# Decoder layer: queries of three kv groups by a seven-product block scheme, weights scaled by a two-scalar instruction

## The chip, the core and the metric

The kernel runs on one core of a Trainium2 chip. The metric is the device time of one launch in microseconds (us). A core has five engines with a queue each: PE (matrix products into PSUM), DVE (VectorE), ACT (ScalarE), POOL (GpSimd, which works on SBUF) and SP, which here issues the DMAs. Each queue runs in its order and waits on semaphores.

## The reference

One decoder layer on `x` of 8 x 128 tokens of 512 columns: causal self-attention with 32 query heads in 8 kv groups of 4, then attention of each sequence to a context, then a gated feed-forward part with 4-bit weights. The self-attention views the 1024 rows of `x` as they come:

```python
q = (hidden_states @ w_q).reshape(B, S, Hkv, g, D)
k = (hidden_states @ w_k).reshape(B, S, Hkv, D)
v = (hidden_states @ w_v).reshape(B, S, Hkv, D)
scores = jnp.einsum('bqhgd,bkhd->bhgqk', q, k) * scale
scores = jnp.where(causal, scores, -jnp.inf)
probs = jax.nn.softmax(scores.astype(jnp.float32), axis=-1).astype(q.dtype)
attn = jnp.einsum('bhgqk,bkhd->bqhgd', probs, v)
return attn @ w_o
x = x + _L0_attn_ref(_layernorm(x, axis=-1), w_q, w_k, w_v, w_o)
x = x + _L0_xattn_ref(ctx_4096, ctx_4096, _layernorm(x, axis=-1))
x = x + _L0_ffn_ref(_layernorm(x, axis=-1), ...)
```

(The kernel has the shapes of the reference's arguments as given: 8 sequences of 128 rows.) Only the projections `q`, `k`, `v`, their weights and the dequantised zeros are touched here.

## The kernel before

**Numbers as pairs.** Every f32 operand of a product is split into two 16-bit parts, hi and lo (`split`, L115: ACT casts to hi, then another engine subtracts for lo). A product of two pairs takes three matmuls, hi*hi, hi*lo, lo*hi (`mm3`, L158). Weights are first scaled by a power of two, so that the 16-bit range holds them: `sumsq` (L242, ACT) and `scales` (L270, one small matmul into bank "a" and a few DVE instructions) find the factor, and `convert` (L348) applies it on POOL (`tensor_tensor` with a broadcast factor, L356), casts on ACT and subtracts on POOL.

**Tokens.** `begin` (L830) loads `x`, normalises it and writes `hT[part][half]`, the normalised tokens transposed, columns of 512 tokens in each of two halves, 4 contraction tiles (KT) of 128 rows. Half 0 is also kept in f32, `h32`, in memory that the feed-forward weights take later.

**Units and steps.** Attention runs over units (kv group g, half), 16 of them, of four sequences each: 64 steps. In step i, `step` (L1368) traces the scores of step i+1 (`att_s`, bank "s"), the projections for the unit of step i+5 (`proj_piece`: k at its first step, one query head a step by `proj_q`, values in two of the four steps, all in bank "j"), the output product of step i-1 (`att_o`, bank "o", added into `xr` by DVE at L665) and the probability product of step i (`att_v`, bank "a"). One `proj_q` is 4 contraction tiles x 3 = 12 matmuls of 128x512, then an ACT cast and a DVE subtraction out of PSUM. PSUM has 8 banks, two for each letter.

**Softmax of one step.** DVE reduces scores out of PSUM (L611), ACT exponentiates (L568), POOL scales by the reciprocal sums (L578, L625), ACT and POOL split into `pb` (L116, L119), SP issues the DMA that transposes `pb` into `pt` (L639); `att_v` waits for `pt`.

**Weights to come.** `todo` holds for each step the loads (`fetch_wq`, `fetch_wk`, `fetch_wv`, `fetch_wo`), squares, factors and splits of later groups. Steps 8 on also dequantise one chunk of the feed-forward weights each (`dequant`). Query weights of a group come as one load of 1 MB into one buffer; k and v weights have buffers of their own.

**Order.** Instructions are traced in the order above; a list scheduler of the framework then orders each engine's queue by its own model of time. `in_order` pins the traced order in `begin` and in the last steps.

## Time and profile before

| what | before |
|---|---|
| median of 3 runs (lowest to highest) | 660.35 us (658.78 to 661.13) |
| span of the profiled execution (the page gives no other time of it) | 659.3 us |
| instructions | 12426 |
| query matmuls of 128x512: L162, L163, L164 | 252 each, 379 to 381 ns a record |
| output-product matmuls: L162, L163, L164 | 256 each, 379 ns a record |
| POOL scalings `rawq`, `rawo`, `rawk`, `rawv` (L356), 128x512 | 28, 30, 7 and 6, at 1048, 1053, 1040 and 1037 ns |
| POOL lo parts `wql`, `wol`, `wkl`, `wvl` (L119) | 1167, 1179, 1155 and 1200 ns |
| granted TensorE clock, mean | 0.995 |
| DMA moved | 69.34 MB, mean 105 GB/s |

How to read the profile: each engine's busy time is the sum of its records; matmul records overlap, since the next matmul enters the array before the one ahead has drained, so the distance between two starts is what a matmul costs and the record's length is its latency. A line of a group gives the code line, the engine, the operation, the tiles it writes and reads with their shapes, the count, then busy time, mean duration, and the idle time before it with what ended that.

### The profile page before, as it was taken

The numbers are of one execution on the slowest core, as the hardware profiler recorded it, in microseconds if no ns is written. First come the engines' busy times: TensorE is split into PE (matmuls) and PEld (weight loads), VectorE is DVE, ScalarE is ACT, GpSimd is POOL, SyncE is SP. The second block draws the span as 40 slices with busy tenths as digits, with TensorE's granted clock in tenths as the row PEclk, the third lists the DMA queues.
The fourth block names the chain that finished last, engine by engine and source line by source line (L and its number), as shares of the span: only waits on it lengthen the run. The fifth ranks groups of instructions, "written<-read, shape, count | busy, mean of one in ns | idle before, by whom it ended". The sixth has DMA issues, their size and how long they took to land.

```text
span 659.3 us, 12426 instructions
## 1 busy us (share of the span) xinstructions
PE 630.6 (96%) x3992; PEld 341.9 (52%) x3992; DVE 469.9 (71%) x1474; ACT 440.4 (67%) x1238; POOL 395.8 (60%) x586
## 2 busy tenths in 40 slices
PE   8789999899999999999999999899998988999996
PEld 5455545455655555565555565456554444445443
DVE  6845786656767776675778565677776768988986
ACT  5676677465758574666677565976566578867674
POOL 7757497664747795556588597663576247622521
PEclk9999999999999999999999999999999999999998
DMA  9277244945553755455547514242544243112002
GB/s 316 54 174 146 84 46 133 229 105 158 121 157 80 192 130 153 109 152 140 144 112 163 149 37 120 46 103 57 90 76 70 41 86 55 22 27 65 1 1 64
DMA packets 117773, 69.34 MB, mean 105 GB/s; under 512 B 84190, under 2 KB 100593, under 8 KB 117708
## 3 DMA queue, kind: packets, MB, share of 16 engines
q1 hardware_dynamic: 117708, 68.55, 43.7%
q8 instruction: 31, 0.51, 0.3%
q14 instruction: 34, 0.28, 0.1%
HBM read 42.12 MB, written 2.20 MB: 67 GB/s over the span
## 4 chain that ended last, share of the span: by engine, by line
PE 56%; POOL 13%; DMA 10%; DVE 8%; issue 7%; ACT 5%; SPq 1%; DVEq 0%; POOLq 0%; ACTq 0%
PE ps_c L1184 6%; PE ps_c L1185 6%; PE ps_o L164 5%; PE ps_o L162 5%; PE ps_o L163 5%; PE ps_q L163 5%; PE ps_q L162 5%; PE ps_q L164 5%; DMA pt<-pb 3%; DMA rawq<-in_L_attn_w_q_dram 3%; POOL pb L119 3%; DMA rawo<-in_L_attn_w_o_dram 2%; POOL s L625 2%; POOL wql L119 1%; POOL rawo L356 1%
## 5 line engine op out<-in xcount | busy, mean ns | idle before, releaser
L568 ACT ACTIVATE s<-s,negm 128x64 f32<-128x64 f32 (+1 forms) x256 | 93.1, 365 | 31.6 <-DVE negm L611 31.3
L162 PE MATMUL ps_o<-woh,ah 128*128 128x512 f16 x256 | 97.1, 379 | 3.2 <-ACT ah L116 3.2
L162 PE MATMUL ps_q<-hT,wqh 128*128 128x512 f16 (+1 forms) x260 | 98.2, 378 | 1.7 <-DVE ql L119 1.7
L163 PE MATMUL ps_q<-hT,wqh 128*128 128x512 f16 (+1 forms) x260 | 98.2, 378 | 0.0
L164 PE MATMUL ps_q<-hT,wql 128*128 128x512 f16 (+1 forms) x260 | 98.0, 377 | 0.0
L164 PE MATMUL ps_o<-woh,al 128*128 128x512 f16 x256 | 96.9, 379 | 0.6 <-DVE al L119 0.6
L163 PE MATMUL ps_o<-wol,ah 128*128 128x512 f16 x256 | 97.0, 379 | 0.0
L119 POOL TENSOR_TENSOR pb<-s,pb 128x256 f16<-128x256 f32 (+1 forms) x128 | 71.7, 575 | 14.8 <-ACT pb L116 12.4
L665 DVE SCALAR_TENSOR_TENSOR xr<-ps_o,unsc,xr 128x512 f32<-128x512 f32 x64 | 47.8, 747 | 42.5 <-PE ps_o L164 41.9
L611 DVE CUSTOM_DVE_ANT_0 s<-ps_sc,mask,soft 128x64 f32<-128x64 f32 (+1 forms) x256 | 66.9, 309 | 4.3 <-PE ps_sc L164 2.0
L578 POOL TENSOR_SCALAR rec<-rec 128x4 f32<-128x4 f32 x64 | 14.8, 231 | 90.1 <-DVE rec L576 87.4
L625 POOL TENSOR_TENSOR s<-s,rec 128x128 f32<-128x128 f32 (+1 forms) x128 | 64.3, 523 | 4.5
L116 ACT CAST pb<-s 128x256 f16<-128x256 f32 (+1 forms) x128 | 43.0, 350 | 33.7 <-POOL s L625 30.0
L119 DVE TENSOR_TENSOR ql<-ps_q,qh 128x512 f16<-128x512 f32 x64 | 43.9, 686 | 28.8 <-ACT qh L116 28.6
L116 ACT CAST ah<-ps_at 128x512 f16<-128x512 f32 x64 | 37.1, 581 | 23.3 <-PE ps_at L164 10.1
L119 DVE TENSOR_TENSOR al<-ps_at,ah 128x512 f16<-128x512 f32 x64 | 43.7, 683 | 7.0 <-ACT ah L116 6.6
L568 ACT ACTIVATION_READ_ACCUMULATOR s<-s,negm 128x1 f32 x256 | 48.1, 188 | 0.0
L116 ACT CAST qh<-ps_q 128x512 f16<-128x512 f32 x64 | 36.7, 573 | 14.0 <-PE ps_q L164 12.5
L1197 DVE TENSOR_SCALAR ps_c<-ps_c,rTg 128x512 f32<-128x512 f32 (+1 forms) x56 | 40.7, 750 | 7.1 <-PE ps_c L1185 6.8
L356 POOL TENSOR_TENSOR rawo<-rawo,sco 128x512 f32<-128x512 f32 x30 | 31.4, 1053 | 22.5 <-DVE sco L312 20.3
L1195 ACT ACTIVATE ps_c<-ps_c,rTu 128x512 f32<-128x512 f32 (+1 forms) x57 | 36.3, 659 | 11.3 <-PE ps_c L1185 9.2
L164 PE MATMUL ps_sc<-k,ql 128*128 128x64 f16 (+1 forms) x256 | 42.7, 206 | 0.5 <-DVE ql L119 0.5
(243 smaller groups left out, 1728.9 us busy)
## 6 DMA issues: line engine op xcount, KB each, us to landing
rawq<-in_L_attn_w_q_dram SPq DMA_DIRECT2D x8, 1024.0 KB
rawo<-in_L_attn_w_o_dram SPq DMA_DIRECT2D x8, 1024.0 KB, 6.0
zi<-zd SPq DMA_DIRECT2D x26, 256.0 KB, 4.1
vd<-v SPq DMA_DIRECT2D x64, 64.0 KB, 2.6
qr<-_L_ffn_down_qweight_dram SPq DMA_DIRECT2D x10, 256.0 KB
xr<-in_x_dram SPq DMA_DIRECT2D x8, 256.0 KB, 7.7
rawk<-in_L_attn_w_k_dram SPq DMA_DIRECT2D x8, 256.0 KB, 4.5
rawv<-in_L_attn_w_v_dram SPq DMA_DIRECT2D x4, 512.0 KB
```

The source lines that it names most:

```text
L116: a = nc.scalar.copy(hi, src)
L119: b = (lo_eng or nc.vector).tensor_tensor(lo, src, hi, ALU.subtract)
L162: nc.tensor.matmul(ps, lh, rh, start=start and i == 0, stop=False)
L163: nc.tensor.matmul(ps, lh, rl, start=False, stop=False)
L164: nc.tensor.matmul(ps, ll, rh, start=False, stop=stop and i == n - 1)
L568: exp = nc.scalar.activation(v, v, AF.Exp, bias=negm[:, j : j + 1], scale=-1.0, accum_out=sums[:, j : j + 1],)
L611: nc.vector.tensor_tensor_reduce(view, flat(ps, cols[j]), masks[j // 2], soft_t[g][:, j % 2 : j % 2 + 1], BIG, ALU.add, ALU.min, negm,)
L625: mul = nc.gpsimd.tensor_tensor(v, v, rec[:, 2 * k : 2 * k + 2].unsqueeze(2).to_broadcast([P, 2, (k + 1) * HQ]), ALU.mult,)
L665: return nc.vector.scalar_tensor_tensor(xr[b], ps, unsc_t[g], xr[b], ALU.mult, ALU.add)
L1184: nc.tensor.matmul(ps, lh, rh, start=r == 0, stop=False, skip_group_check=r > 0)
L1185: nc.tensor.matmul(ps, lh, rl, start=False, stop=True, skip_group_check=r > 0)
L1197: nc.vector.tensor_scalar(ps, ps, sc, None, ALU.mult)
```

## The change

Three things are changed.

**Seven products.** For kv groups 3, 4 and 5 (`FAST`), the queries of two heads (a pair p of a group) over both halves are seen as a 2x2 block product: two heads by two halves of the contraction (2 of the 4 tiles each), times two halves of the contraction by two token halves. Instead of eight block products of 6 matmuls (`proj_q` four times), `fast_q` makes seven, with sums of weight blocks (`fast_prep`, part 2, four DVE additions; Z0 and Z1 are their pairs) and sums of token blocks (`t_part`, once, in steps 8 to 11; kept as pairs in `tT`). Partial products are shared: an ACT copy puts half of c11 into the bank of `u`, on which PE goes on adding, and DVE adds `s5`, the fifth product, to `u` twice. `fast_q` is cut in four parts by its yields, and `fast_steps` runs them in successive steps, 8g-9 to 8g-6 for the first pair and 8g-5 to 8g-2 for the second (the third part of the very first pair comes in step 18, with the fourth). All four query tiles of a pair come in these steps, half 1 long before its use, so those of the second pair's half 1 are kept in a pool of their own (`tp`, beside `tT`).

**Scaling.** `scaled` applies a weight's factor on POOL by `tensor_scalar` with two per-partition scalars, `nil` (zero, added) and the factor, in place of the `tensor_tensor`.

**Room and order for it.** Scores have one bank "s", and "b" is the bank of `u`; where no `u` is live, scores alternate between both (tag "sb"). Query weights come in two loads of 512 KB, k and v weights share one buffer, and their loads, squares and splits move; group 1's k load moves within `begin`. Value projections of later groups go to bank "o", one in each of 8 steps. Work tiles of the start (`warm`, `hb`, `h`, the first k weights, zeros and scales) move into memory of the feed-forward weights (`lent`), the zeros are stored as 16-bit numbers, both masks share a tile, and `junk` is 8 bits wide.

```diff
-    BANKS = {"j": 2, "s": 2, "a": 2, "o": 2}
+    BANKS = {"j": 2, "s": 1, "a": 2, "o": 2, "b": 1}
+
+    flip = [0]
     def bank(tag, shape, name):
+        if tag == "sb":
+            flip[0] += 1
+            tag = "bs"[flip[0] % 2]
...
-    def fetch_wq(g, pieces=((0, GH),)):
-        src = wq[:, g * TH : (g + 1) * TH].rearrange("(kt p) d -> p kt d", p=P)
-        raw_t["q", g] = raw = rawp.tile([P, KT, TH], F32, name="rawq", tag="rawq", bufs=1)
-        for a, b in pieces:
-            nc.sync.dma_start(raw[:, :, a * P : b * P], src[:, :, a * P : b * P])
+    def fetch_wq(g, pairs=(0, 1)):
+        for p in pairs:
+            c0 = g * TH + p * 2 * P
+            raw_t["q", g, p] = raw = rawp.tile([P, KT, 2 * P], F32, name="rawq", tag="rawq")
+            nc.sync.dma_start(
+                raw, wq[:, c0 : c0 + 2 * P].rearrange("(kt p) d -> p kt d", p=P)
+            )
+
+    def raw_q(g, j):
+        return raw_t["q", g, j // 2][:, :, j % 2 * P : (j % 2 + 1) * P]
+
+    def raw_kv(shape, name):
+        return rawp.tile(shape, F32, name=name, tag="rawkv", bufs=1)
...
+        raw = k0_raw if g == 0 else raw_kv([P, KT, P], "rawk")
...
+    def scaled(raw, sc):
+
+        return nc.gpsimd.tensor_scalar(raw, raw, nil, sc, ALU.add, ALU.mult)
+
     def convert(hi, lo, raw, sc, direct=False):
         if direct:
             a = nc.scalar.activation(hi, raw, AF.Copy, scale=sc)
             b = nc.vector.scalar_tensor_tensor(lo, raw, sc, hi, ALU.mult, ALU.subtract)
             return a, b
-        wide = sc
-        while len(wide.shape) < len(raw.shape):
-            wide = wide.unsqueeze(2)
-        a = nc.gpsimd.tensor_tensor(
-            raw, raw, wide.to_broadcast(list(raw.shape)), ALU.mult
-        )
+        a = scaled(raw, sc)
...
+    def lent(m, at, n, dt=F16, rows=P):
+
+        view = nfflat[m][:rows, at : at + n]
+        return view if dt == F16 else view.bitcast(dt)
+    warm = lent("g", 0, TH)
+    hbs = [lent("g", TH + i * 2 * H, 2 * H).rearrange("p (a t) -> p a t", a=2) for i in range(HB)]
+    k0_raw = lent("u", 0, 2 * KT * P, F32).rearrange("p (k d) -> p k d", k=KT)
+    tmp32 = [
+        lent("u", i * 4 * TH, 4 * TH, F32).rearrange("p (k t) -> p k t", k=2) for i in range(2)
+    ]
+    wide32 = lent("d", 2 * HB * H, 2 * TH, F32).rearrange("p (b t) -> p b t", b=HB)
...
-        ps = transpose4(ln_t.pop(("h", b)), "s" if b == 2 else "o")
+        ps = transpose4(ln_t.pop(("h", b)), "ojso"[b])
...
-        if j % 2 == 0:
-            q_t[g, half, j // 2] = [
-                qp.tile([P, HB, 2, 2, HQ], F16, name="q" + p, tag="q" + p) for p in "hl"
-            ]
-        hi, lo = q_t[g, half, j // 2]
         for cs in pieces:
             proj(ps[:, cs], wq_t[g * GH + j], half, cs)
             yield
+        put_q(g, half, j, ps)
+        yield
+
+    EXTRA = 2
+    FAST = range(3, 6)
+    extra = [(g, 1, 1) for g in FAST]
+
+    def put_q(g, half, j, ps):
+        key = g, half, j // 2
+        if key not in q_t:
+
+            q_t[key] = [
+                tp.tile([P, HB, 2, 2, HQ], F16, name="q" + p, tag="x" + p, bufs=EXTRA)
+                if key in extra
+                else qp.tile([P, HB, 2, 2, HQ], F16, name="q" + p, tag="q" + p)
+                for p in "hl"
+            ]
+        hi, lo = q_t[key]
         split(
             hi[:, :, :, j % 2, :],
             lo[:, :, :, j % 2, :],
             ps.rearrange("p (b a t) -> p b a t", a=2, t=HQ),
         )
+
+
+    tT = tp.tile([P, 2, 4, 2, TH], F16, name="T")
+
+    def t_part(i):
+
+        low, high = slice(0, 2), slice(2, KT)
+        one, two = tmp32
+        hh, hl = hT[0][1], hT[1][1]
+        if i == 0:
+            nc.vector.tensor_tensor(one, hh[:, low, :], h32[:, low, :], ALU.subtract)
+            nc.vector.tensor_tensor(one, one, hl[:, low, :], ALU.add)
+            src = one
+        elif i == 1:
+            nc.vector.tensor_tensor(two, hh[:, high, :], one, ALU.subtract)
+            nc.vector.tensor_tensor(two, two, hl[:, high, :], ALU.add)
+            src = two
+        elif i == 2:
+            nc.vector.tensor_tensor(one, two, h32[:, low, :], ALU.subtract)
+            src = one
+        else:
+            nc.vector.tensor_tensor(one, h32[:, high, :], two, ALU.subtract)
+            src = one
+        split(tT[:, 0, i], tT[:, 1, i], src, nc.gpsimd)
+
+    s_w = {}
+
+    def fast_raw(g, p):
+        return raw_t["q", g, p].rearrange("p k (i d) -> p k i d", i=2)
+
+    def fast_units(key, raw, kts=slice(0, KT)):
+        n = raw.shape[1]
+        hi = wqp.tile([P, KT, P], F16, name="wqh", tag="wqh")
+        lo = wqp.tile([P, KT, P], F16, name="wql", tag="wql")
+        s_w[key] = hi, lo
+        a, b = split(hi[:, KT - n :, :], lo[:, KT - n :, :], raw, nc.gpsimd)
+
+    def fast_prep(g, p, part):
+
+        raw = fast_raw(g, p)
+        a, b = slice(0, 2), slice(2, KT)
+        if part < 2:
+            j = 2 * p + part
+            mine = raw[:, :, part, :]
+            issue_after(scaled(mine, sc_t["q", g][:, j : j + 1]), pace["mul"])
+            fast_units((g, p, "XY"[part]), mine if part == 0 else mine[:, b, :])
+        elif part == 2:
+            a11, a12, a21, a22 = raw[:, a, 0, :], raw[:, b, 0, :], raw[:, a, 1, :], raw[:, b, 1, :]
+            tt = nc.vector.tensor_tensor
+            tt(a22, a21, a22, ALU.add)
+            tt(a21, a11, a21, ALU.subtract)
+            tt(a11, a22, a11, ALU.subtract)
+            tt(a12, a12, a11, ALU.subtract)
+        else:
+            fast_units((g, p, "Z0"), raw[:, :, 0, :])
+            fast_units((g, p, "Z1"), raw[:, :, 1, :])
+
+    def fast_q(g, p):
+
+
+
+
+        X, Y, Z0, Z1 = (s_w.pop((g, p, n)) for n in ("X", "Y", "Z0", "Z1"))
+        first, last = slice(0, 2), slice(2, KT)
+
+        def term(ps, w, k0, rhs, start):
+            mm = nc.tensor.matmul
+            for k in range(2):
+                wh, wl = w[0][:, k0 + k, :], w[1][:, k0 + k, :]
+                rh, rl = rhs[0][:, k, :], rhs[1][:, k, :]
+                new = start and k == 0
+                mm(ps, wh, rh, start=new, stop=False, skip_group_check=not start)
+                mm(ps, wh, rl, start=False, stop=False, skip_group_check=not start)
+                mm(ps, wl, rh, start=False, stop=k == 1, skip_group_check=not start)
+
+        def tok(half, part):
+            return [hT[i][half][:, part, :] for i in range(2)]
+
+        def summed(i):
+            return tT[:, 0, i], tT[:, 1, i]
+
+        m5 = bank("j", [P, TH], "ps_q5")
+        term(m5, Z1, 2, summed(0), True)
+        s5 = work.tile([P, TH], F32, name="s5", tag="s5", bufs=1)
+        nc.scalar.copy(s5, m5)
+        if (g, p) == (FAST[0], 0):
+            wet = bank("b", [P, TH], "ps_w")
+            nc.tensor.matmul(wet, X[0][:, 0, :], hT[0][0][:, 0, :], start=True, stop=True)
+        c11 = bank("j", [P, TH], "ps_q1")
+        term(c11, X, 0, tok(0, first), True)
+        u = bank("b", [P, TH], "ps_qu")
+        nc.scalar.copy(u, c11)
+        yield
+        term(c11, X, 2, tok(0, last), False)
+        put_q(g, 0, 2 * p, c11)
+        term(u, Z0, 0, summed(1), False)
+        c12 = bank("j", [P, TH], "ps_q2")
+        nc.vector.tensor_tensor(c12, u, s5, ALU.add)
+        yield
+        term(u, Z1, 0, summed(2), False)
+        nc.vector.tensor_tensor(s5, u, s5, ALU.add)
+        term(c12, Z0, 2, tok(1, last), False)
+        put_q(g, 1, 2 * p + 1, s5)
+        put_q(g, 1, 2 * p, c12)
+        yield
+        term(u, Y, 2, summed(3), False)
+        put_q(g, 0, 2 * p + 1, u)
...
-    def proj_v(pr, b):
+    def proj_v(pr, b, place="j"):
         half, bb = divmod(b, HB)
         cs = slice(bb * P, (bb + 1) * P)
-        ps = bank("j", [P, 2 * P], "ps_v")
+        ps = bank(place, [P, 2 * P], "ps_v")
...
-        ps = bank("s", [P, 6, HQ], "ps_sc")
+        apart = not FAST[0] - 1 <= g < NG - 3
+        ps = bank("sb" if apart else "s", [P, 6, HQ], "ps_sc")
...
-        zt["d"] = dram.tile([NZ, INTER], I32, name="zd")
-        nc.sync.dma_start(zt["d"], zt["z"].rearrange("p a e -> p (a e)"))
+        z16 = lent("u", 3104, INTER, rows=NZ)
+        nc.vector.tensor_copy(z16, zt["z"].rearrange("p a e -> p (a e)"))
+        zt["d"] = dram.tile([NZ, INTER], F16, name="zd")
+        nc.sync.dma_start(zt["d"], z16)
...
-        fetch_wk(1)
         prep_wv(0, 1, True)
+        fetch_wk(1)
...
+    fast_steps = {}
+    fast_last = []
+    for g in FAST:
+        for p in range(2):
+            base = 8 * g - 9 + 4 * p
+            where = [base, base + 1, base + 2, base + 3]
+            if (g, p) == (FAST[0], 0):
+                where = [base, base + 1, base + 3, base + 3]
+            fast_last.append(where[-1])
+            box = []
+
+            def stage(g=g, p=p, box=box):
+                if not box:
+                    box.append(fast_q(g, p))
+                next(box[0])
+
+            for i in where:
+                fast_steps.setdefault(i, []).append(stage)
+    for i, b in zip((39, 40, 41, 42), range(HB)):
+        fast_steps.setdefault(i, []).append(lambda b=b: run(proj_v((NG - 2) // 2, b, "o")))
+    for g in (2, 4):
+        for b in range(B):
+            fast_steps.setdefault(8 * g - 5 + b, []).append(
+                lambda g=g, b=b: run(proj_v(g // 2, b, "o"))
+            )
...
+        if g not in FAST:
+            run(proj_q(g, half, j))
+        yield
+        if (u < 2 or u == len(units) - 2) and j in (1, 2):
...
+            at(m - 4, lambda g=g: fetch_wv(g // 2))
+            at(m - 3, lambda g=g: sumsq("v", g // 2, 0, 0))
+            at(m - 2, lambda g=g: scales("v", g // 2))
+            at(m - 1, lambda g=g: prep_wv(g // 2, 0))
+            at(m, lambda g=g: prep_wv(g // 2, 1))
         if g > 1:
+            at(c - 4, lambda g=g: fetch_wk(g))
+            at(c - 3, lambda g=g: sumsq("k", g, 0, 0))
+            at(c - 2, lambda g=g: scales("k", g))
+        if g in FAST:
+            for p in range(2):
+                to = 8 * g - 13 + 4 * p
+                up = to - (2 if (g, p) == (FAST[0], 0) else 4)
+                both = 2 * p, 2 * p + 2
+                at(up, lambda g=g, p=p: fetch_wq(g, (p,)))
+                at(to - 2, lambda g=g, p=p: sumsq("q", g, 0, 2 * p))
+                at(to - 1, lambda g=g, p=p: sumsq("q", g, 0, 2 * p + 1))
+                at(to - 1, lambda g=g, both=both: scales("q", g, both))
+                for part in range(4):
+                    at(to + part, lambda g=g, p=p, part=part: fast_prep(g, p, part))
+            at(8 * g - 9, lambda g=g: soft_scale(g))
+        elif g > 1:
             m = c - HB
-            at(m, lambda g=g: fetch_wk(g))
-            at(m + 1, lambda g=g: (fetch_wq(g), sumsq("k", g, 0, 0)))
+            at(m + 1, lambda g=g: fetch_wq(g))
             at(m + 2, lambda g=g: (sumsq("q", g, 0, 0), sumsq("q", g, 0, 1)))
             at(m + 3, lambda g=g: (sumsq("q", g, 0, 2), sumsq("q", g, 0, 3)))
-            at(m + 3, lambda g=g: (scales("q", g), scales("k", g), soft_scale(g)))
-        for j in range(GH):
-            at(c + j, lambda g=g, j=j: prep_wq(g, j))
-        at(c + 1, lambda g=g: prep_wk(g))
+            at(m + 3, lambda g=g: (scales("q", g), soft_scale(g)))
+        if g not in FAST:
+            for j in range(GH):
+                at(c + j, lambda g=g, j=j: prep_wq(g, j))
+        at(c, lambda g=g: prep_wk(g))
...
-            c = HB * (u0 - 3)
-            at(c - 2, lambda g=g: fetch_wv(g // 2))
-            at(c - 1, lambda g=g: sumsq("v", g // 2, 0, 0))
-            at(c, lambda g=g: scales("v", g // 2))
-            at(c + 2, lambda g=g: prep_wv(g // 2, 0))
-            at(c + 3, lambda g=g: prep_wv(g // 2, 1))
...
-    ring = ["j", "s", "o"]
+    ring = ["j", "sb", "o"]
...
         proj_piece(*divmod(i + 1 + HB, HB))
+        for f in fast_steps.pop(i, ()):
+            f()
...
+        if 8 <= i < 12:
+            t_part(i - 8)
```

## The prediction

> **What bounds the kernel now.** I read the page's busy shares first, then the stretches of the trace in which the change works, then TensorE's timeline inside them, then its waits.
>
> ```profile
> span 659.3 us, 12426 instructions
> PE 630.6 (96%) x3992; PEld 341.9 (52%) x3992; DVE 469.9 (71%) x1474; ACT 440.4 (67%) x1238; POOL 395.8 (60%) x586
> ```
>
> PE looks like the bound, but a record of a 512-wide matmul is 379 ns long while the next starts sooner, so the share alone proves nothing. The stretch table places it (core, then sum (count) by engine, clock, DMA):
>
> ```profile
> core 0: us, PE busy (x) PEld busy (x) DVE busy (x) ACT busy (x) POOL busy (x), PEclk, DMA share, GB/s
> 102.60:133.50 30.90, 29.15 (x197) 15.79 (x196) 20.16 (x75) 20.50 (x68) 20.21 (x30) 1.00 0.64 158
> 133.50:157.70 24.20, 24.20 (x167) 14.61 (x165) 14.27 (x44) 14.99 (x46) 15.42 (x23) 1.00 0.44 105
> 157.70:347.10 189.40, 188.82 (x1260) 105.39 (x1258) 130.99 (x427) 121.43 (x395) 124.25 (x187) 1.00 0.55 140
> ```
>
> A step of the schedule ends in one accumulation into `xr` (L665), and counting these puts steps 8 to 11 at about 102.6 to 133.5 us, steps 12 to 14 in the second row and steps 15 to 38 in the third. The seven-product work lies in the third, where PE is busy 99.7% at full clock and DVE, ACT and POOL have 58, 68 and 65 us free. Is PE also dense there? Its timeline:
>
> ```profile
> 320.34 0.38 PE L162 MATMUL ps_q<-hT,wqh 128*128 128x512 f16 x1
> 320.55 0.38 PE L163 MATMUL ps_q<-hT,wqh 128*128 128x512 f16 x1
> ...
> 322.71 0.38 PE L164 MATMUL ps_q<-hT,wql 128*128 128x512 f16 x1
> 322.93 0.19 PE L162 MATMUL ps_sc<-k,qh 128*128 128x64 f16 x1
> ```
>
> Twelve matmuls of one query tile take 322.93 - 320.34 = 2.59 us: one starts each 0.216 us. That, not 0.379, is what a matmul costs. Subtracting each matmul's own spacing from the gaps between starts, I find only some 1.4 us lost in the whole of the third stretch. So PE paces it, and fewer matmuls shorten the kernel until something else comes up. The waits of PE name what could:
>
> ```profile
> PE ps_at L648 <- DMA pt<-pb: 4.2, 6, 1.7
> PE ps_v L162 <- DVE ql L119: 3.4, 3, 2.5
> PE ps_o L162 <- ACT ah L116: 3.2, 3, 2.6
> ```
>
> (us in all, times, longest): softmax, whose end on POOL releases the `pt` transpose, and evacuations of PSUM.
>
> **The products.** Before, a pair of query heads takes 2 heads x 2 halves x 12 = 48 matmuls. After: Z1 (6), X (6+6), Z0 (6), Z1 (6), Z0 (6), Y (6) = 42. Six pairs save 36, and one matmul is added (`wet`): 35 x 0.216 = **-7.55 us** on the path. Three more calls of `scales` add three one-column matmuls, under 0.1 us.
>
> **Work on the other engines.** Prices are these rows (busy us, mean ns, idle before):
>
> ```profile
> L116 ACT CAST qh<-ps_q 128x512 f16<-128x512 f32 x64 | 36.7, 573 | 14.0 <-PE ps_q L164 12.5 <-PE ps_n L287 1.5
> L119 DVE TENSOR_TENSOR ql<-ps_q,qh 128x512 f16<-128x512 f32 x64 | 43.9, 686 | 28.8 <-ACT qh L116 28.6
> L119 POOL TENSOR_TENSOR wql<-rawq,wqh 128x512 f16<-128x512 f32 x28 | 32.5, 1167 | 0.8 <-ACT wqh L116 0.8
> L356 POOL TENSOR_TENSOR rawq<-rawq,scq 128x512 f32<-128x512 f32 x28 | 29.2, 1048 | 16.0 <-DVE scq L312 15.7 <-DVE sb L283 0.3
> L116 ACT CAST wqh<-rawq 128x512 f16<-128x512 f32 x28 | 17.1, 616 | 7.7 <-POOL rawq L356 7.5
> L548 DVE SCALAR_TENSOR_TENSOR v<-ps_v,v 128x256 f16<-128x256 f32 x32 | 13.3, 417 | 6.2 <-ACT v L547 5.9
> L1002 POOL TENSOR_SCALAR h<-xr,rs,rstd 128x512 f32<-128x512 f32 x16 | 12.3, 767 | 1.2
> L351 DVE SCALAR_TENSOR_TENSOR cp<-c,scx,cp 128x512 f16<-128x512 f32 x8 | 8.4, 1046 | 2.0 <-ACT cp L350 2.0
> ```
>
> Per pair on DVE: four weight sums of 256 columns with both inputs in SBUF. No such row exists; the nearest of that width is L548, 0.42, and the bounds are 0.35 (half of ql) and 0.52 (half of L351, two SBUF inputs): 4 x 0.42 = 1.7. Two additions to `u` at ql's 0.69: 1.4. Together 3.1 us a pair, 18.5 for six; 16 to 23 by the bounds.
> Per pair on ACT: hi halves 3.5 tile widths instead of 2, 1.5 x 0.616 = 0.9; the copies to `s5` and `u`, 2 x 0.57 = 1.15. Together 2.1, for six 12.4.
> Per pair on POOL: lo halves, 1.5 x 1.167 = +1.75; two scalings by the two-scalar form at L1002's price, 2 x (0.767 - 1.048) = -0.56. Together +1.2, for six +7.1. The scalings of the other weights in this stretch (some 20 on k, v and o) give back 20 x 0.28 = 5.6.
> Against the free 58, 68 and 65 us these fit: DVE goes to (131 + 18.5) / 182 = 82%, ACT to 74%, POOL to 69%. On the path: nothing, as long as matmuls lie between a hand-over and its use; if that cover is gone, the fourth rival below has the price.
>
> **The token sums** (`t_part`, steps 8 to 11). DVE: six operations of 1024 columns, about 2 x 0.75 (L351 undisturbed, at 12.85 us of the timeline) = 1.5 each, 9 us; bounds 8.2 (twice ql) and 12.6 (twice the mean L351). ACT 4 x 1.05 (junk<-rawo, 1024 wide) = 4.2; POOL 4 x 2 x 1.167 = 9.3. The first row of the stretch table has 10.7 us free on DVE and 10.7 on POOL, so both come to about 95%; nothing needs T before step 15, and the next stretch has 9.9 and 8.8 free. But each sum is 1.5 to 2.3 us long on an in-order queue, with the query split, `al`, the score reductions and the softmax parts behind it, and PE behind those; PE already waited 1.7 us once for `pt` there. I take **+1.2 us**, bounds 0 and 5 (four steps of one 1.2 us wait each, about half of the longest such wait, 2.5).
>
> [...]
>
> **Hand-overs inside a pair.** PE waits for ACT (`u` copied from half of c11), for DVE (`u + s5` into c12, before Z1 is added to u), and again for DVE (`s5` from u, before Y). Each is a step apart, except in the first pair, where the last two parts share step 18: six matmuls (1.3 us) then cover an addition of 0.69 and its queue. Queued behind such a wait on PE is everything of that step: scores, the output product, `att_v`. **+0.7 us**, bounds 0 and 10 (rival). Scores of groups 2 to 4 get one bank instead of two: the reduction ends 1.4 to 3.1 us after the last score matmul, and steps are 7.9 us apart, so this costs nothing unless two score sets follow at once; within the same +0.7.
>
> **Start and other moves.** Query weights come in two loads of 512 KB; the first squares waited 0.24 us for theirs, so at most -0.24. The load of k weights of group 1 is moved in SP's queue ahead of two transposes, behind `wvl` ending at 27.7 us; the later transpose follows hb at 31.3, so it hides it. Value weights share one buffer with k weights: load, squares and splits come one to three steps sooner than their use needs, but a load that waits for its buffer would hold the `pt` transposes behind it on SP. POOL's 1.5 us of memsets move out of the idle start. Zeros in 16 bits halve 35 loads and add one DVE copy of about 1.4 us. Value products move to bank "o", which holds one output product a step. I put **0** on all of these, bounds -1 and +2. Faster scalings shorten a wo chain near 422 us (rawo x3, 3.44 us, then a 2.8 us gap of PE): **-0.3**, bounds -0.8 and 0.
>
> **Sum.** -7.55 + 0.1 + 1.2 + 0.7 + 0 - 0.3 = -5.85; I round the stalls up to have **-5.4 us**. Against this execution's span 659.3: 653.9. The median shown, 660.35, lies 1.1 above the span: **655.0 us**.
>
> **Rivals.** (a) *All of it arrives*: stalls 0 and the start a little quicker, -7.6 to -10: 650 to 652.8. For it: only 1.4 us lost in the stretch; against: T burst. (b) *Other engines come up*: POOL or DVE paces the bursts (in single steps near 245, 340 and 365 us POOL is all but full), so two thirds to all of the gain goes: 658.4 to 662. Against: such steps cost PE almost nothing before. (c) *The new scheme doesn't shorten PE*, since weight loads pace it: 660; PEld is busy 56% there with 512-wide matmuls as before, so I count it within (b). (d) *Slower, by the hand-overs*: PE runs in order, so each of 6 x 3 hand-overs may stop it if the order puts its user right behind. A wait like the score reductions' lag less an addition's cover, about 1 us, gives 18 - 7.55 = +10: 670. It eats the gain from 7.55 / 18 = 0.42 us a hand-over, and decides for slower from 0.53. For it: an evacuation waits typically 1.4 us and more; against: the steps between.
>
> **How the numbers follow.** Forecast 0.60 (652.8 to 658.4), (a) 0.12, (b) with (c) 0.14, (d) 0.14. A measurement of this kernel tells about 0.3%, 2.0 us, from no change. Faster 0.72 plus 0.01 from the edge of (b), same 0.13, slower 0.14. The range reaches from 650.5 into (b): 661.5.
>
> **What would show it.** PE's count of 512-wide query matmuls down by 36 and a spacing still 0.216; the stretch of steps 15 to 38 about 7 us shorter with PE still above 98% busy; POOL scaling near 0.77; DVE at some 82% there. Wrong if PE waits for `ps_q` evacuations, `u` or `s5` show more than 4 us in sum, if weight sums take over 0.6 us, or if `pt` waits in steps 8 to 12 pass 5 us.

## The result, and the profile after

The changed kernel takes 683.15 us (682.63 to 683.9, four runs) against 660.74 us (658.78 to 661.49) of the kernel before in the same comparison: 1.0345 times as long, 95% interval 1.0318 to 1.0371. The forecast was 655.0. The page after, span and busy time of each engine:

```profile
span 681.6 us, 12453 instructions
PE 627.9 (92%) x3960; PEld 339.4 (50%) x3960; DVE 498.7 (73%) x1530; ACT 451.1 (66%) x1264; POOL 409.1 (60%) x599
```

Next to the lines of before: PE has 32 records fewer and is busy for less of a longer span, 92% against 96%. No engine has come up to take its place, so PE now waits more. The stretch table by the same count of accumulations into `xr`: steps 8 to 11, 12 to 14, 15 to 38, and, not shown of before, 39 to 43 (before: 38.17 of 38.30 us):

```profile
107.80:141.10 33.30, 27.04 (x173) 14.24 (x171) 20.86 (x69) 21.34 (x67) 23.40 (x35) 1.00 0.58 127
141.10:163.80 22.70, 22.70 (x160) 13.58 (x158) 15.88 (x56) 15.92 (x51) 19.23 (x28) 1.00 0.50 115
163.80:366.20 202.40, 194.98 (x1306) 108.43 (x1305) 149.04 (x483) 134.35 (x423) 124.59 (x189) 0.99 0.47 115
366.20:413.90 47.70, 39.38 (x268) 22.15 (x266) 31.77 (x107) 31.54 (x109) 34.04 (x57) 0.96 0.50 127
```

PE has holes in the first, third and fourth. To weigh them I take from every gap between two matmul starts the first one's own spacing (0.216 us for 512 columns, in proportion for others: about 0.11 for 256 and 0.03 for 64 in the timeline). The rest is PE's loss; the spacings themselves sum to PE's work. (The 80 transposes of f32 are counted at 0.216 too, though their starts lie 0.11 apart. That takes about 5 us of loss from the first column and 3 from the last, in every row alike, so the differences between rows stand.) Work went from 626.3 to 618.8 us, loss from 26.8 to 56.3. By steps, each counted up to the first matmul of its `att_v`, for the two kernels and the runs told below:

| run | 0-3 | 4-14 | 15-25 | 26-37 | 38-43 | 44-59 | 60-end | loss | work |
|---|---|---|---|---|---|---|---|---|---|
| before | 7.1 | 3.0 | 0.2 | 0.7 | 0.0 | 8.2 | 7.7 | 26.8 | 626.3 |
| changed | 6.0 | 11.6 | 6.7 | 3.4 | 10.5 | 5.0 | 13.1 | 56.3 | 618.8 |
| no sevens | 6.1 | 2.0 | 0.0 | 0.4 | 0.0 | 6.7 | 11.8 | 27.0 | 626.3 |
| no token sums | 6.0 | 2.6 | 7.1 | 2.3 | 11.9 | 4.9 | 13.1 | 47.9 | 618.8 |
| paced sums | 6.4 | 9.1 | 6.9 | 2.7 | 10.2 | 4.6 | 12.8 | 52.7 | 618.8 |
| own k buffer | 7.4 | 2.3 | 3.2 | 2.5 | 7.4 | 7.0 | 14.3 | 44.1 | 618.8 |
| values later | 6.2 | 2.6 | 6.9 | 2.7 | 5.4 | 4.6 | 12.9 | 41.3 | 618.8 |
| free banks, no sevens | 5.6 | 3.2 | 0.0 | 0.4 | 0.9 | 6.8 | 7.9 | 24.8 | 626.3 |
| the same, early queries | 5.1 | 1.9 | 0.0 | 0.4 | 5.1 | 4.7 | 7.6 | 24.8 | 626.3 |
| all mended | 5.6 | 9.5 | 3.3 | 1.5 | 7.9 | 5.3 | 8.8 | 41.9 | 618.6 |

What PE waited for in the changed kernel (us in all, times, longest):

```profile
PE ps_at L799 <- DMA pt<-pb: 15.8, 11, 2.6
PE ps_o L162 <- ACT ah L116: 4.6, 4, 2.1
PE ps_o L164 <- DVE al L119: 3.1, 4, 2.1
PE ps_qu L630 <- DVE ps_q L656: 2.9, 1, 2.9
...
PE ps_c L1377 <- DVE pr L1410: 2.0, 3, 1.0
PE ps_c L1377 <- ACT sg L1405: 1.9, 2, 1.4
```

`pt` waits grew from 4.2 to 15.8 us; the fourth row is a hand-over inside a pair, which happened once; the last two are of the feed-forward chains. So four places lose time, and in only one of them does a product wait for a product. Three are followed here in their own lines, the feed-forward part with its run below.

**Steps 5 to 8: the token sums.** They are traced in steps 8 to 11, but the list scheduler issued them from 84 to 107 us, in steps 5 to 8 as the table counts (5 to 7 by accumulations into `xr`). There DVE already had zeros and scales to prepare. Two windows, then some of DVE's and POOL's timelines (start, length):

```profile
80.50:96.50 16.00, 13.85 (x89) 6.97 (x87) 16.00 (x35) 10.19 (x33) 15.73 (x17) 1.00 0.14 28
96.50:116.00 19.50, 14.91 (x90) 7.43 (x91) 18.47 (x61) 14.67 (x49) 19.10 (x22) 1.00 0.29 88
```

```profile
90.67 2.12 DVE L573 TENSOR_TENSOR nfu<-hT,nfu 128x1024 f32<-128x1024 f16 x1
...
94.72 1.21 DVE L574 TENSOR_TENSOR nfu<-nfu,hT 128x1024 f32<-128x1024 f32 x1
...
97.20 1.21 DVE L577 TENSOR_TENSOR nfu<-nfu,nfd 128x1024 f32<-128x1024 f32 x1
```

```profile
90.55 1.16 POOL L119 TENSOR_TENSOR wol<-rawo,woh 128x512 f16<-128x512 f32 x1
91.83 2.94 POOL L119 TENSOR_TENSOR T<-nfu,T 128x1024 f16<-128x1024 f32 x1
94.75 1.27 POOL L728 TENSOR_SCALAR rec<-rec 128x4 f32<-128x4 f32 x1
...
97.20 1.93 POOL L363 TENSOR_SCALAR rawo<-rawo,nil,sco 128x512 f32<-128x512 f32 x1
```

DVE is busy 16.00 of 16.00 us, POOL 15.73. And in three places the two did not overlap as they seem to. A sum that ran freely took 1.21. The scaling of four columns, 0.22 elsewhere, took 1.27 when it came 0.03 after a sum; the scaling of 512, 0.77 elsewhere, took 1.93 when it came with one: nearly its own length and the rest of the sum's (0.22 + 1.18 = 1.40, 0.77 + 1.21 = 1.98). The sum of L573 came 0.12 after POOL's `wol`, and took 2.12, where 1.21 + 1.04 make 2.25. In all three, one of the two took its own length and what was left of the other, to 0.13 us. Softmax has its parts on both engines, and `pt` came late: three waits, 3.4 us, up to 105 us. (A fourth, of 2.6 us, is at 130 us in step 10, where the kernel without the sums, told below, loses 2.1 us too.) The largest single wait of these steps came behind the last low half:

```profile
109.47 2.12 POOL L119 TENSOR_TENSOR T<-nfu,T 128x1024 f16<-128x1024 f32 x1
```

```profile
109.83 2.90 DVE L342 TENSOR_SCALAR soft<-scq,sck 64x2 f32<-64x2 f32 x2
```

```profile
113.51 0.39 PE L164 MATMUL ps_o<-woh,al 128*128 128x512 f16 x1 [2.09 <-DVE al L119]
```

Two scalings of two columns (0.21 us at the shortest of the 16) stood 2.90 us on DVE until POOL had ended that low half and the split of `wkl` behind it (at 112.70 us); `al` was queued after them, and PE waited 2.09 us for it.

**Steps 20 to 24: a late load.** DVE, then one line each of POOL, SP, ACT, and PE:

```profile
220.00 0.41 DVE L608 TENSOR_TENSOR rawq<-rawq 128x256 f32<-128x256 f32 x1
221.62 0.16 DVE L296 CAST sb<-ssk 128x1 bf16<-128x1 f32 x1 [1.22 <-ACT junk L273]
221.70 0.82 DVE L967 SCALAR_TENSOR_TENSOR nfu<-qi,zi 128x512 f16<-128x512 int32 x1
222.44 1.37 DVE L609 TENSOR_TENSOR rawq<-rawq 128x256 f32<-128x256 f32 x1
223.85 0.53 DVE L610 TENSOR_TENSOR rawq<-rawq 128x256 f32<-128x256 f32 x1
224.30 0.69 DVE L656 TENSOR_TENSOR ps_q<-ps_qu,s 128x512 f32<-128x512 f32 x1
```

```profile
216.15 1.15 POOL L119 TENSOR_TENSOR wvl<-rawv,wvh 128x512 f16<-128x512 f32 x1
```

```profile
217.33 0.38 SPq L239 DMA_DIRECT2D rawk<-in_L_attn_w_k_dram  x1
```

```profile
220.87 0.63 ACT L273 ACTIVATE junk<-rawk 128x512 uint8<-128x512 f32 x1 [2.81 <-DMA rawk<-in_L_attn_w_k_dram]
```

```profile
225.04 0.59 PE L630 MATMUL ps_qu<-T,wqh 128*128 128x512 f16 x1 [2.87 <-DVE ps_q L656]
225.42 0.63 PE L631 MATMUL ps_qu<-T,wqh 128*128 128x512 f16 x1
```

Read backwards: PE waits 2.87 us for `c12` (L656). It stood on DVE behind three weight sums, an unpacking and a one-element cast of the k weights' squares. The cast stood 1.22 us for ACT, ACT for a load, and the load was issued at 217.33 because the last reader of the shared k and v buffer, `wvl`, ended at 217.30.

**Steps 39 to 42: values parked in banks.** The first two value products of groups 6 and 7 on PE, the `att_v` of step 40, and the evacuations of those two on ACT:

```profile
358.57 0.27 PE L162 MATMUL ps_v<-wvh,hT 128*128 128x256 f16 x1
...
369.87 0.27 PE L162 MATMUL ps_v<-wvh,hT 128*128 128x256 f16 x1
...
375.45 0.37 PE L799 MATMUL ps_at<-pt,vd 128*128 128x256 f16 x1 [1.41 <-DMA pt<-pb]
```

```profile
376.79 0.38 ACT L697 ACTIVATE v<-ps_v 128x256 f16<-128x256 f32 x1
...
383.79 0.38 ACT L697 ACTIVATE v<-ps_v 128x256 f16<-128x256 f32 x1 [1.36 <-PE ps_at L164]
```

The first product lay 17 us in its bank. Its result goes to the buffer of a value of groups 4 and 5 that `att_v` of step 40 still reads; the second waited for step 41 in the same way. From 370 to 378 us both banks "o" were held, and the output products had none.

### The profile page after: what moved, and what is told of

Its sections match the earlier page's. It is cut to its first block, busy times and chain, and to the rows that moved or that the text cites. A ratio compares the mean times of both kernels' runs of the same rounds, so it can differ in the third digit from the quotient of the medians.

```text
span 681.6 us, 12453 instructions
## 1 busy us (share of the span) xinstructions
PE 627.9 (92%) x3960; PEld 339.4 (50%) x3960; DVE 498.7 (73%) x1530; ACT 451.1 (66%) x1264; POOL 409.1 (60%) x599
## 4 chain that ended last, share of the span: by engine, by line
PE 46%; DVE 16%; POOL 13%; DMA 11%; ACT 7%; issue 6%; SPq 0%; DVEq 0%; POOLq 0%; ACTq 0%
PE ps_c L1377 6%; PE ps_c L1378 6%; PE ps_o L162 4%; PE ps_o L164 4%; PE ps_o L163 4%; DMA pt<-pb 3%; PE ps_q L162 2%; PE ps_q L164 2%; PE ps_q L163 2%; DVE ps_c L1390 2%; POOL pb L119 2%; POOL wql L119 2%; POOL s L776 2%; DMA c<-in_ctx_dram 2%; DMA rawq<-in_L_attn_w_q_dram 2%
## 5 line engine op out<-in xcount | busy, mean ns | idle before, releaser
L119 POOL TENSOR_TENSOR pb<-s,pb 128x256 f16<-128x256 f32 (+1 forms) x128 | 74.2, 594 | 24.9 <-ACT pb L116 22.7
L728 POOL TENSOR_SCALAR rec<-rec 128x4 f32<-128x4 f32 x64 | 18.1, 283 | 88.0 <-DVE rec L726 65.1
L776 POOL TENSOR_TENSOR s<-s,rec 128x128 f32<-128x128 f32 (+1 forms) x128 | 65.8, 534 | 4.2
L116 ACT CAST pb<-s 128x128 f16<-128x128 f32 (+1 forms) x128 | 43.1, 348 | 31.5 <-POOL s L776 26.2
L162 PE MATMUL ps_q<-hT,wqh 128*128 128x512 f16 (+1 forms) x164 | 61.3, 374 | 1.7 <-DVE ql L119 1.7
L164 PE MATMUL ps_q<-hT,wql 128*128 128x512 f16 (+1 forms) x164 | 61.3, 374 | 0.0
L163 PE MATMUL ps_q<-hT,wqh 128*128 128x512 f16 (+1 forms) x164 | 61.3, 374 | 0.0
L119 DVE TENSOR_TENSOR ql<-ps_q,qh 128x512 f16<-128x512 f32 x52 | 35.6, 684 | 23.4 <-ACT qh L116 23.4
L119 POOL TENSOR_TENSOR wql<-rawq,wqh 128x512 f16<-128x512 f32 (+1 forms) x40 | 43.9, 1110 | 5.3 <-ACT wqh L116 5.2
L164 PE MATMUL ps_sc<-k,ql 128*128 128x64 f16 (+1 forms) x256 | 41.9, 206 | 1.2 <-DVE ql L119 1.2
L164 PEld LDWEIGHTS <-al 128*128 128x128 f16 x256 | 25.0, 98 | 33.6 <-DVE al L119 6.4
```

The source lines that it names most:

```text
L116: a = nc.scalar.copy(hi, src)
L119: b = (lo_eng or nc.vector).tensor_tensor(lo, src, hi, ALU.subtract)
L162: nc.tensor.matmul(ps, lh, rh, start=start and i == 0, stop=False)
L163: nc.tensor.matmul(ps, lh, rl, start=False, stop=False)
L164: nc.tensor.matmul(ps, ll, rh, start=False, stop=stop and i == n - 1)
L776: mul = nc.gpsimd.tensor_tensor(v, v, rec[:, 2 * k : 2 * k + 2].unsqueeze(2).to_broadcast([P, 2, (k + 1) * HQ]), ALU.mult,)
```

## The experiments

Times are compared by their ratios to the kernel before as measured beside them; a difference of 0.001 is 0.66 us.

**The scaling alone**, in the kernel before.

```diff
-        wide = sc
-        while len(wide.shape) < len(raw.shape):
-            wide = wide.unsqueeze(2)
-        a = nc.gpsimd.tensor_tensor(
-            raw, raw, wide.to_broadcast(list(raw.shape)), ALU.mult
-        )
+        a = nc.gpsimd.tensor_scalar(raw, raw, nil, sc, ALU.add, ALU.mult)
```

> The kernel before with the two-scalar scaling alone. Theory (the loss comes with the seven products and their room): POOL scalings drop from 1.05 to about 0.77 us each, PE waited little for them, so 657 to 661 us. Rival (any change of POOL's times reorders the queues and costs by itself): 664 us or more, with the time lost by PE in steps 4 to 43 well above the 8 us of before.

Measured: 660.08, ratio 0.9993 (0.9978 to 1.0008). The scalings shrank from about 1.05 to 0.77 to 0.79 us, and the time stayed: POOL isn't waited for here.

**Score banks in turns**, in the kernel before.

```diff
-    BANKS = {"j": 2, "s": 2, "a": 2, "o": 2}
+    BANKS = {"j": 2, "s": 1, "a": 2, "o": 2, "b": 1}
...
+        if tag == "sb":
+            flip[0] += 1
+            tag = "bs"[flip[0] % 2]
```

> The kernel before with one change: the two banks of tag s become single banks b and s that scores and feed-forward chains take in strict turns. Theory (the tail of the changed kernel loses 5 us more because a chain waits for its turn's bank): 664 to 667 us, the loss behind step 55. Rival (turns cost nothing, the tail's loss comes from another place): 659 to 662 us.

Measured: 664.5, ratio 1.0066 (1.0049 to 1.0083). Waits for `ps_c` in the feed-forward part, of the kernel before and of this run:

```profile
PE ps_c L1184 <- ACT sg L1212: 1.1, 1, 1.1
...
PE ps_c L1184 <- DVE pr L1217: 0.5, 2, 0.3
```

```profile
PE ps_c L1189 <- DVE pr L1222: 2.0, 3, 1.0
PE ps_c L1189 <- ACT sg L1217: 1.9, 2, 1.4
```

The second pair is that of the changed kernel to the digit. A chain that must take the bank whose turn it is waits for that one's reader, whether or not the other stands free. About 4 of the 5.4 us that the changed kernel loses more after step 60 are this and no product.

**No seven products**: everything else of the change.

```diff
-    FAST = range(3, 6)
+    FAST = ()
-        if 8 <= i < 12:
-            t_part(i - 8)
```

> The changed kernel with no group under the seven products (no token sums, no weight sums; loads, buffers, banks and scaling as changed; scores always alternate between banks s and b). Theory (the seven products and the token sums cause the stalls): PE work up by 7.5 us, the 22 us of extra stalls in the attention steps gone, the 5 us more in the tail kept: about 666 us, 660 to 669. Rival (the moved loads, the shared buffer and the banks cause them): 683 + 7.5, about 690 us.

Measured: 661.15, ratio 1.0012 (1.0001 to 1.0022), loss 27.0. The moved loads, the shared buffer, the value products in "o" and the turns together cost next to nothing while queries are made as before; what the turns take after step 60, smaller losses before it give back. The rest of the 22 us needs the seven products to come about, with their sums, their early queries and the one score bank of groups 2 to 4, for which this run gives scores both banks in turn. No run takes that one bank by itself.

**No token sums**: the products stay.

```diff
-            return tT[:, 0, i], tT[:, 1, i]
+            return tok(i % 2, (first, last)[i // 2])
```

> The changed kernel without the token sums: products that would read them read token blocks instead, so queries of groups 3 to 5 are not the reference's. Theory (the sums were drawn forward into the steps where DVE was already busy and fill it from 73 to 113 us of the span): the 8.4 us more that PE loses in steps 4 to 11 go, 675 us, 672 to 677. Rival (DVE is full there for other reasons, the shared k and v buffer that delays the value load): 681 to 684 us.

Measured: 673.15, ratio 1.0197 (1.017 to 1.0223), 9.8 us under the changed kernel. Loss in steps 4 to 14 falls from 11.6 to 2.6, elsewhere it stays. A part forecast at 1.2 us takes 10.

**Token sums in their own steps.**

```diff
+        for t in sums:
+            issue_after(t, after)
-            t_part(i - 8)
+            t_part(i - 8, paced)
```

> The changed kernel, whole, but each VectorE operation of t_part is given an order-only dependency on the output accumulation of its own step (8 to 11), so that no sum can be issued ahead of the step it is written in. If the 10 us that the sums cost come from their place (they ran at 84 to 107 us, in steps 4 to 7, where VectorE was already full), TensorE's loss in steps 4 to 11 goes from about 10 us above the kernel before to 2 or less and the time to 673 to 677. Rival: the sums cost the same wherever they stand, because VectorE and POOL stretch each other's instructions: 680 to 685, with the loss moved into steps 8 to 12.

Measured: 677.5 (671.9 to 680.58), ratio 1.0232 (1.017 to 1.0295). Between the two: 7.5 us less by the ratios, loosely (3 to 12 by their intervals; the profiled execution's loss is 3.6 less). Steps 4 to 8 are healed (so the sums' place did cost there), but steps 11 to 13 now lose 7.8 us where the kernel without the sums loses 0.3. Lines of DVE and POOL of this run:

```profile
126.72 2.17 DVE L578 TENSOR_TENSOR nfu<-nfu,nfd 128x1024 f32<-128x1024 f32 x1
128.81 2.44 DVE L970 SCALAR_TENSOR_TENSOR nfg<-qi,zi 128x352 f16<-128x352 int32 x1
```

```profile
127.77 5.46 POOL L119 TENSOR_TENSOR T<-nfu,T 128x1024 f16<-128x1024 f32 x2
```

```profile
131.97 0.27 PE L802 MATMUL ps_at<-pt,vd 128*128 128x256 f16 x1 [3.04 <-DVE r L309]
```

The unpacking of 352 columns took 0.52 us at this place in the run without sums, 2.44 here; two low halves took 5.46 for an undisturbed 4.24. Behind the sum and the unpacking on DVE stood `r`, which reads a weight factor out of a bank "a", and `att_v` of step 11 waited 3.04 us for that bank: the largest piece of the 7.8. So the place is one part of the price, and the blocking came along at the second place too.

**A k buffer of its own**, on top of the kernel without token sums.

```diff
-        raw = k0_raw if g == 0 else raw_kv([P, KT, P], "rawk")
+        raw = k0_raw if g == 0 else rawp.tile([P, KT, P], F32, name="rawk", tag="rawk")
```

> The changed kernel without the token sums (the products read plain token halves, so the queries of groups 3 to 5 are wrong by what T would have added; 673.2 us so far), and with a buffer of its own for the k weights in place of the one shared with the value weights. In steps 20 to 24 a one-element cast (sb from ssk) stood 1.5 us on VectorE for squares whose load had waited for the shared buffer, with weight sums and the sum into c12 queued behind it, and TensorE then waited 3.0 us for c12. Theory: the late load is the cause of TensorE's loss of 6.4 us in steps 21 to 24; it goes below 2 us and the time to 667 to 669. Rival: the hand-over is late by VectorE's own queue, with or without the cast: 672 to 674.

Measured: 671.13, ratio 1.0145 (1.0114 to 1.0175), some 3.4 us less (0.7 to 6 by the intervals). The cast and `c12` in this run:

```profile
210.81 0.16 DVE L296 CAST sb<-ssk 128x1 bf16<-128x1 f32 x1 [0.43 <-ACT junk L273]
...
214.92 0.69 DVE L655 TENSOR_TENSOR ps_q<-ps_qu,s 128x512 f32<-128x512 f32 x1
```

The cast stands 0.43 us where it stood 1.5 with the shared buffer, and PE's wait for `c12` is gone; steps 21 and 22 lose 0.9 us in place of 4.9. The time is above the 667 to 669 forecast for the late load and under the rival's 672: the wait was the late load's, its price was put too high. Elsewhere the traced execution differs in both directions, 4.5 us less loss in steps 38 to 43, 4.7 more in steps 0 to 3 and from 44 on, which no run traces to the buffer.

**Values later**, on the same kernel.

```diff
-    for i, b in zip((39, 40, 41, 42), range(HB)):
+    for i, b in zip((43, 44, 45, 46), range(HB)):
```

> The changed kernel without the token sums (as in the run before this one; 673.2 us), and with the value products of groups 6 and 7 four steps later (43 to 46 in place of 39 to 42). At 39 to 42 they are written before the value buffer they need is free, so they stand in both banks of tag o until att_v of the next step has run, and the output products wait for a bank. Theory 1: these parked banks are TensorE's loss of 12 us in steps 38 to 43: it goes below 4 us and the time to 663 to 667. Theory 2: these steps are short of matmuls, since the queries of the second half of group 5 are done four steps sooner than before, so taking four value products away too makes them no better: 672 to 676.

Measured: 667.43, ratio 1.009 (1.0061 to 1.0118), 7.1 us less; loss in steps 38 to 43 falls from 11.9 to 5.4, to none from step 41 on. Theory 1 holds for that part; time and loss both end a little above what it gave (667 us, 4 us), since steps 39 and 40 keep 5.4.

**Early queries without sevens.** `proj_q(5, 1, j)` at step 35 + j instead of 39 + j, two query tiles in extra buffers.

> No seven products at all and no token sums (all queries by eight products, as in the run at 661.2 us); the only difference to that run is that the queries of the second half of group 5 are done in steps 35 to 38 in place of 39 to 42, where the seven-product scheme has them too. TensorE's work is that of before. Theory 2 (steps 39 to 42 are short of matmuls, so that softmax paces them): TensorE loses 6 to 12 us in steps 39 to 43 and the time is 667 to 673. Rival (hand-overs, parked banks or weight preparation alone): 660 to 663.

Measured: 662.83, ratio 1.0025 (1.0005 to 1.0044). A miss for theory 2 as priced; the time lies in the rival's range. Steps 41 to 46 lose 4.5 us more than in the run at 661.15, steps 48 to 52 lose 2.9 less, and the 0.9 us by the ratios is not told from nothing.

**Free banks and late values, no sevens.**

```diff
-    BANKS = {"j": 2, "s": 1, "a": 2, "o": 2, "b": 1}
+    BANKS = {"j": 2, "s": 2, "a": 2, "o": 2}
-    ring = ["j", "sb", "o"]
+    ring = ["j", "s", "o"]
```

> No seven products (as in the run at 661.2 us: two-scalar scaling, moved loads, shared buffer), with the two score banks given out as they come free, as in the kernel before, in place of strict turns, and the value products of groups 6 and 7 at steps 43 to 46. Strict turns alone cost the kernel before 4 us, most of it in the feed-forward tail. Theory (the costs are separate and add): TensorE's loss from step 60 on goes from 12.2 us to about 8 and the time to 655 to 659, under both kernels. Rival (something else ends last in the tail): 660 to 662.

Measured: 659.08 (twelve runs), ratio 0.9969 (0.9948 to 0.9989): 0.3% under the kernel before, and so under both. Loss after step 60 is back at 7.9.

**All four mended, with sevens**: paced sums, k weights of groups 2 to 5 in lent space, late values, free banks (`u` in one of them).

> The whole change with the four causes found so far taken out: token sums paced to steps 8 to 11, k weights of groups 2 to 5 in a buffer of their own (in space lent by the down weights), value products of groups 6 and 7 four steps later, and both score banks given out as they come free, u among them. Separate causes that add: 683.2 - 5.7 - 2 to 3.5 - 5.7 - 4 = 664 to 666, by measured differences; range 662 to 668, still above the kernel before. Rival (the losses stand in for each other, and u standing in a score bank for three steps makes scores wait): 670 to 678. Seven products would only pay if it came under 658.

Measured: 667.39, ratio 1.0104 (1.0068 to 1.014): 15.9 us of the 22.4 are back. That is in the range, 1.4 us above the 664 to 666 that the parts add up to, and the seven products still don't pay. Against the row above with free banks, 7.7 us less work stand against 17.1 more loss: 6.3 in steps 4 to 14, 3.3 in 15 to 25, 1.1 in 26 to 37, 7.0 in 38 to 43.

**Low halves of the token sums on VectorE**, in the mended kernel.

```diff
-        split(tT[:, 0, i], tT[:, 1, i], src, nc.gpsimd)
+        split(tT[:, 0, i], tT[:, 1, i], src)
```

> The mended kernel of the run before (667.4 us), with one line changed: the low half of each token sum is subtracted on VectorE (about 1.2 us each) in place of POOL (2.1 to 3.1 us each). What is left of the sums' cost there is a loss of 8.4 us in steps 11 to 14, where the kernel without the seven products loses none after step 10. Theory (POOL's long operations and VectorE's lock each other out: an unpacking of 0.68 us took 2.44 beside such a low half): the loss in steps 11 to 14 goes below 5 us and the time to 662 to 665. Rival (VectorE is simply full in these steps, so 5 us more on it costs as much again): 667 to 671.

Measured: 666.38, ratio 1.0092 (1.0063 to 1.0121): not told from the run before. Steps 11 to 14 lose 6.8 us in place of 8.4. The wait for `r` there fell from 3.0 to 0.9 us, with the unpacking back at 0.51, so for that one wait the theory holds. In its place `pt` came late three times, for 2.3 us in all, where it had been once, for 1.0. Neither forecast of the time is met.

**Early queries again**, in the 659.1 us kernel.

> The 659.1 us kernel of the run before (no seven products, free banks, values late) with the queries of the second half of group 5 done in steps 35 to 38 in place of 39 to 42, as the seven-product scheme has them. The mended kernel still loses 7.9 us in steps 38 to 43. Theory (these steps are left with too few matmuls to cover softmax, whatever the products are): TensorE loses 4 to 8 us in steps 39 to 44 here too, the time is 662 to 666. Rival (the loss belongs to the seven products: their hand-overs and splits): under 1.5 us there, 658 to 661.

Measured: 661.68, ratio 1.002 (1.0004 to 1.0035) against 0.9969 (0.9948 to 0.9989): 3.4 us more by the medians (1.7 to 5 by the intervals), a little under the forecast. The trace places it only in part: the profiled execution is the fastest of the ten, 659.03, and its loss in all is 24.8, as without early queries. It loses 5.1 us in steps 38 to 43 where the other lost 0.9, and gives that back in other steps. What PE waits for in steps 38 to 43:

```profile
PE ps_q L164 <- POOL wql L119: 2.2, 1, 2.2
PE ps_q L162 <- ACT wqh L116: 0.7, 1, 0.7
```

PE, done with group 5 early, comes to group 6 while POOL is still splitting its weights. With the query matmuls of these steps gone, little covers that, nor a softmax that is late.

## Why the prediction was wrong, step by step

**PE's work** was forecast 7.55 us down and went down by 7.5. Right, and it is the only gain.

**Work on the other engines** in steps 15 to 38 was right as well: DVE 131 + 18.5 = 149.5 forecast, 149.04 in the third row above; ACT 133.8 and 134.35; POOL 125.7 and 124.59. DVE's share is 74% and not 82 because the stretch became 202 us long. Weight sums and scalings as groups (busy us, mean ns):

```profile
L608 DVE TENSOR_TENSOR rawq<-rawq 128x256 f32<-128x256 f32 x6 | 2.5, 417 | 0.4 <-POOL wql L119 0.4
L609 DVE TENSOR_TENSOR rawq<-rawq 128x256 f32<-128x256 f32 x6 | 3.7, 620 | 0.1
L363 POOL TENSOR_SCALAR rawq<-rawq,nil,scq 128x512 f32<-128x512 f32 x28 | 22.0, 793 | 8.3 <-DVE scq L325 8.3
```

An undisturbed weight sum takes the 0.42 forecast; one sum of 1.37, the one shown at 222 us, lifts its row to 0.62. **Rival (b)** falls in its form: no engine is full over the stretch, and the burst that did fill DVE and POOL cost more than the whole gain. **Rival (c)** falls with PE's work, which did go down.

**The token sums** were the step that failed first. Their own price was right (six DVE operations 8.2 us, forecast 9; four low halves on POOL 9.3, forecast 9.3), but "+1.2 us, bounds 0 and 5" was made for steps 8 to 11 with 10.7 us free on DVE. The operations need nothing from step 8 or later, and this list scheduler issued them ahead, from step 5 on, where DVE was busy 16.00 of 16.00 us. The run without them puts the price at 9.8 us. The forecast also let DVE and POOL run side by side there, and by the lines above they did not: on DVE a sum of 1.21 took 2.12, on POOL a scaling of 0.77 took 1.93. The kernel before has one such row: L351 took 0.75 us at 12.85 us and 1.32 at 26.43, where it came 0.38 after a POOL subtraction of 1.15.

**"I put 0 on all of these, bounds -1 and +2"** failed next, and cost more. The turns of the score banks take 4.4 us (ratio 1.0066) in the feed-forward part, which I hadn't priced, since the banks were named there only for scores. That "a load that waits for its buffer would hold the `pt` transposes" named the shared buffer's danger in the wrong place: it held a cast on DVE, for 3.4 us. Value products in bank "o", "which holds one output product a step", take 7.1: I counted tenants and not how long each stays.

**"+0.7 us" for hand-overs inside a pair.** Of 18, one stopped PE, the one behind the late cast. Rival (d) thus has the right side and, at 670, about half of the loss, but by a mechanism that the runs don't show. Alone it wouldn't have decided: 2.9 us of wait and some 1.5 at a lowered clock, against 7.5.

**A step that wasn't there**: the scheme makes both halves of a group's queries at once, so the second half's come four steps sooner, and the steps that lose them stand bare. That is 3.4 us by the medians of the last run, 0.9 and not told from nothing in the earlier pair, and part of the 7.0 us that steps 38 to 43 of the mended kernel still lose.

**The signs** set for being wrong watched other places: `pt` waits in steps 8 to 12 came to 2.6 us of the 5 named, and of the weight sums one row just passed 0.6, at 0.62. No sign was set for steps 5 to 7, the score banks, the shared buffer or the parked values.

By measured differences 9.8 + 4.4 + 3.4 + 7.1 + 3.4 make 28.1 us; 7.5 us of work and 3.2 of loss in steps 44 to 59 (8.2 to 5.0) go off, which leaves 17.4 of the 22.4. The differences were taken on different kernels and stand in for one another in part (the four mended together gave 15.9, singly about 22), so the sum is a rough account and no proof that nothing is missing. Open remain some 6 us of token sums in their own steps, of which 3.0 are the wait for `r` and which moving the low halves did not settle, and single losses of 1.5 us in steps 24 and 29, which no run took apart.

## What to carry to other kernels

Where PE is 99% dense, a saving of matmuls is bounded by what they covered: ask, for each stretch that loses matmuls, which late transfer or split they hid, and for each stretch that gains other work, when it becomes ready, not where it is written. A change of buffers costs the time that a tenant stays, so price each new sharing by its longest stay and follow what is queued behind it, through every part of the kernel that draws on the same banks. Test the arrangement without the idea (here 661.15) and the idea without its preparation (673.15) before tuning either.

## What the hardware showed unasked

After the 3 us hole at 222 us PE came back at half clock: the two matmuls shown start 0.38 us apart where 0.216 is usual, and the window over them grants 0.50.

```profile
225.00:226.60 1.60, 1.56 (x4) 0.54 (x4) 1.60 (x5) 0.27 (x1) 1.02 (x1) 0.50 0.27 56
374.84:378.25 3.41, 2.80 (x10) 1.35 (x10) 1.63 (x11) 3.41 (x13) 3.41 (x7) 0.50 0.33 92
```

Seven matmuls paid 0.21 us each, so this hole cost half as much again as it lasted. The starts on its two sides lie 3.1 us apart (221.96 and 225.04 us), and in the microsecond ahead of it only score matmuls and one `att_v` ran. The second row is another fall of the clock in this kernel: its first matmul started 1.62 us after the one before it, and from 369.28 us on no two starts were further apart. Starts 2.47 us apart, at 111.04 and 113.51 us, left the clock at 1.00. What sets off a fall these rows don't show.
